# Group statistics of a convolution and state-space kernel: from VectorE's bn_stats to ScalarE's accumulating passes, with the group norms cut into stages

## The chip, the cores and the metric

The kernel runs on one core of a Trainium2 chip. The metric is the device time of one execution in microseconds. The engines are named as the profile names them: PE (TensorE, matmul), PEld (its weight load), DVE (VectorE), ACT (ScalarE), POOL (GpSimd), and SP, whose queue issues most DMAs.

## The reference

Two residual layers work on x of shape (2, 768, 64, 64), in float32:

```python
x = x + _L0_conv_ref(_gn(x), ...)   # layer 0
x = x + _L1_conv_ref(_gn(x), ...)   # layer 1
```

`_gn` is a group norm: each of 32 groups of 24 channels, over all 64 x 64 pixels of an image, has its mean taken away and is divided by sqrt(variance + 1e-5). Layer 0 projects 768 channels to 1536, runs a depthwise 3x3 convolution and SiLU, computes from the result (x_proj) a step size (through softplus) and the vectors B and C of a state-space model with 4 states per channel, scans that model over the 4096 pixels in order, adds D*u, normalizes over channels and projects back to 768. Layer 1 goes through a real 2-D Fourier transform, a two-layer block-diagonal complex MLP with a soft threshold, and the inverse transform.

So statistics per channel are needed three times outside layer 0's first input: of the second image's x (before layer 0 starts on that image), and of layer 0's output of each image (before layer 1).

## The kernel before

**Tiling.** Channels lie on the 128 partitions: 768 are NCT = 6 tiles (`ct`), 1536 are NDT = 12 tiles (`dt`). The 4096 pixels of an image are NCH = 16 chunks of T = 256 (four rows). Layer 0 works through 32 chunks, the 16 of image 0 and then those of image 1.

**Slots.** Layer 0's order is written out by hand (`tc.manual_schedule`). A loop runs over slots t; there are 12 per chunk, 384 in all, and 33 more for the pipeline to drain. In slot t the pieces of a software pipeline are issued for different tiles: `project` (L245, input projection) for tile t, `conv` (L284) and `taps` (L297) for t - 2, `delta` (L341 matmul, L345 Softplus) and `decay` (L352, four exponentials per tile) some 15 behind, `scan` (L369 multiplication, L373 scan), `read` (L382, L383) and `gather` (L388, L390) 17 behind, `output` (L444, output projection) 31 behind, each `ct` in two slots (h = 0 and 1), and `finish` (L455 to L460) in the slot after its second half, so in every odd slot. Every engine takes its instructions strictly in this order.

**Phases.** ScalarE's tables are switched in groups of three slots, phase = t % 3. In phase 2 it runs `root` (L430, L431, once per chunk) and then `silu` (L309) for three tiles; in phase 0 it loads Softplus' table, runs L345 three times, loads the table of Ln and Exp (L551) and starts the exponentials, of which eight fall into phase 1. In the last three slots of a chunk it also normalizes the next chunk's input (L226). `x_proj` (L315) is issued in a phase 2, once per chunk; `x_dbl` (L325) and `spread` (L329, L331) follow in the phase 0 behind it. `moments` (L405) sums for the channel norm in phase 1; `variance` (L420, L422) and `spread_of_tokens` (L427) follow once per chunk.

**Buffers.** PSUM: `pi`, `pc` and `pz` have two banks each, `po` and `mom` one. `pz` serves L341, x_proj, L329, L420 and the group norms in turn. So the third L341 of a phase 0 waits until the first L345 has emptied its bank, and the next `output` waits until L455 has read `po`.

**Statistics.** `prepare` (before the slots) takes bn_stats of image 0's input on DVE (L169). Image 1's input comes in 48 slabs of 128x512: `load_slab` (L147) in slots 40 to 87, `slab_stats` (L150, bn_stats on DVE) one slot later, so in slots 41 to 88. `input_norm(1)` runs whole at the end of slot 91. The output's statistics are a bn_stats (L459) in every `finish`; `aggregate` (L135, six bn_aggr) and the group norm run at the end of slot 223 for image 0 and of slot 415 for image 1.

**The group norm** (L58 to L91) goes back and forth between engines: PE sums the channel means over groups (L64), DVE copies (L77), PE spreads them to the channels (L72), DVE forms the variance parts (L79 to L83), PE sums again (L64), ACT takes Ln and Exp (L87, L88), PE spreads (L72), DVE copies (L90).

**The tail.** From slot 390 on, layer 1's first transform of image 0 (`forward_w`, L616) is issued in pieces between layer 0's last slots: L501 normalizes on ACT, L631 transposes, L639 transforms, and L496/L498 evict on DVE and ACT.

Of the kernel before, what the change touches and what calls it, by code (L numbers as in the profile page):

```python
# [9 lines left out]
F32 = mybir.dt.float32  # L10
AF = mybir.ActivationFunctionType
ALU = mybir.AluOpType
# [3 lines left out]
B, DM, H, W = 2, 768, 64, 64  # L16
L = H * W
DI, NS, R = 1536, 4, 48
G, GC = 32, 24
NCT, NDT = DM // 128, DI // 128  # L20
ROWS = 4
T = ROWS * W
NCH = H // ROWS
# [8 lines left out]
def spectral_kernel(tc, a, out):  # L32
    nc = tc.nc
    x = a["x"]
    xr = x.rearrange("b (ct p) h w -> b p ct (h w)", p=128)
    outr = out.rearrange("b (ct p) h w -> b p ct (h w)", p=128)

    with ExitStack() as top:
        dram = top.enter_context(tc.tile_pool(name="dram", bufs=1, space=DRAM))
        cst = top.enter_context(tc.tile_pool(name="cst", bufs=1))  # L40

        x1_d = [dram.tile([128, NCT, L], F32, name=f"x1_{b}") for b in range(B)]
        y_d = [dram.tile([H, W, DP], F32, name=f"yspec_{b}") for b in range(B)]
        v_d = [dram.tile([H, W, DM], F32, name=f"vspec_{b}") for b in range(B)]

        ident = cst.tile([128, 128], F32, name="ident")
        make_identity(nc, ident)
        sel = cst.tile([128, NCT, G], F32, name="sel")
        nc.sync.dma_start(sel, a["c_sel"])
        selT = cst.tile([G, NCT, 128], F32, name="selT")  # L50
        nc.sync.dma_start(selT, a["c_selT"])
        eps = cst.tile([128, 1], F32, name="eps")
        nc.vector.memset(eps, EPS)

        gm1 = [cst.tile([128, NCT], F32, name=f"gm1_{b}") for b in range(B)]
        gr1 = [cst.tile([128, NCT], F32, name=f"gr1_{b}") for b in range(B)]

        def group_norm(mv, mean, rstd, pool, psum, name):  # L58


            def over_groups(cols, what):
                g = psum.tile([128, 512], F32, tag="pz", name=f"{name}_{what}_g")
                for ct in range(NCT):
                    nc.tensor.matmul(  # L64
                        g[:G, 0:1], sel[:, ct, :], cols(ct), start=(ct == 0), stop=(ct == NCT - 1)
                    )
                return g

            def to_channels(vals, what):
                c = psum.tile([128, 512], F32, tag="pz", name=f"{name}_{what}_c")  # L70
                for ct in range(NCT):
                    nc.tensor.matmul(c[:, ct : ct + 1], selT[:, ct, :], vals, start=True, stop=True)  # L72
                return c

            g = over_groups(lambda ct: mv[:, ct, 0:1], "m")
            gs = pool.tile([G, 1], F32, tag="gn_g", name=f"{name}_gm")
            nc.vector.tensor_copy(gs, g[:G, 0:1])  # L77
            c = to_channels(gs, "m")
            nc.vector.tensor_copy(mean, c[:, :NCT])  # L79
            d = pool.tile([128, NCT], F32, tag="gn_d", name=f"{name}_d")  # L80
            nc.vector.tensor_sub(d, mv[:, :, 0], mean)
            nc.vector.tensor_mul(d, d, d)
            nc.vector.tensor_add(d, d, mv[:, :, 1])  # L83
            g = over_groups(lambda ct: d[:, ct : ct + 1], "v")
            sd = pool.tile([G, 1], F32, tag="gn_g", name=f"{name}_sd")

            nc.scalar.activation(sd, g[:G, 0:1], AF.Ln, bias=eps[:G])  # L87
            root = nc.scalar.activation(sd, sd, AF.Exp, scale=-0.5)  # L88
            c = to_channels(sd, "v")
            nc.vector.tensor_copy(rstd, c[:, :NCT])  # L90
            return root.ins  # L91

        with ExitStack() as ctx:
            layer0(ctx, tc, a, xr, x1_d, y_d, ident, group_norm, gm1, gr1, eps)
        with ExitStack() as ctx:
            layer1(ctx, tc, a, x1_d, y_d, v_d, outr, ident, gm1, gr1)


def layer0(ctx, tc, a, xr, x1_d, y_d, ident, group_norm, gm1, gr1, eps):

    nc = tc.nc
    dram = ctx.enter_context(tc.tile_pool(name="dram0", bufs=1, space=DRAM))
    wp = ctx.enter_context(tc.tile_pool(name="w0", bufs=1))
    st = ctx.enter_context(tc.tile_pool(name="st", bufs=1))
    ps = ctx.enter_context(tc.tile_pool(name="ps0", bufs=2, space=PSUM))
# [19 lines left out]
    gm0 = [st.tile([128, NCT], F32, name=f"gm0_{b}") for b in range(B)]  # L125
    gr0 = [st.tile([128, NCT], F32, name=f"gr0_{b}") for b in range(B)]
    gn0 = [st.tile([128, NCT], F32, name=f"gn0_{b}") for b in range(B)]
    stats1 = st.tile([128, NCT, NCH, 6], F32, name="stats1")
    stats0 = st.tile([128, NCT, 8, 6], F32, name="stats0")
    state = st.tile([128, NDT, NS], F32, name="state")  # L130

    def aggregate(stats, n, mean, rstd, name, pool):
        mv = pool.tile([128, NCT, 2], F32, tag="mv", name=f"mv_{name}", bufs=1)
        for ct in range(NCT):
            nc.vector.bn_aggr(mv[:, ct, :], stats[:, ct, :n, :])  # L135
        group_norm(mv, mean, rstd, pool, ps, name)

    def input_norm(b, pool):
        aggregate(stats0, 8, gm0[b], gr0[b], f"gn0_{b}", pool)
        nc.vector.scalar_tensor_tensor(gn0[b], gm0[b], -1.0, gr0[b], ALU.mult, ALU.mult)  # L140

    slabs = {}

    def load_slab(b, n):
        ct, k = divmod(n, 8)
        slabs[n] = p2.tile([128, 512], F32, tag="xs", name=f"xs_{b}_{n}")
        nc.sync.dma_start(slabs[n], xr[b, :, ct, k * 512 : (k + 1) * 512])  # L147

    def slab_stats(n):
        nc.vector.bn_stats(stats0[:, n // 8, n % 8, :], slabs.pop(n))  # L150

    def prepare():
        with tc.tile_pool(name="xi", bufs=3) as xi, tc.tile_pool(name="wi", bufs=1) as wi:
# [10 lines left out]
            for n in range(2 * NCT):  # L164
                ct, h = divmod(n, 2)
                xs = slabs0[n] if n < 3 else xi.tile([128, 2048], F32, tag="xs", name=f"xs0_{n}")
# [20 lines left out]
            for h in range(2):  # L187
# [5 lines left out]
                    )  # L193
                for dt in range(NDT):
                    nc.vector.tensor_sub(wout[:, dt, half], wout[:, dt, half], wm[:, :384])
            input_norm(0, wi)
            for ct in range(NCT):
                nc.gpsimd.dma_start(
                    wout_d[ct].rearrange("p (dt c) -> p dt c", c=128),
# [2 lines left out]

    p2 = ctx.enter_context(tc.tile_pool(name="p2", bufs=2))
    prepare()
    p1 = ctx.enter_context(tc.tile_pool(name="p1", bufs=1))

    class Chunk:
# [244 lines left out]
        def finish(self, ct):  # L452
            b, i = self.b, self.i
            o = p2.tile([128, T], F32, tag="o", name=f"o_{self.n}_{ct}")
            nc.vector.tensor_mul(o, self.po[ct][:, :T], self.rs)  # L455
            nc.vector.scalar_tensor_tensor(
                o, o, obias[:, ct : ct + 1], self.out[ct][1], ALU.add, ALU.add
            )
            nc.vector.bn_stats(stats1[:, ct, i, :], o)  # L459
            nc.sync.dma_start(x1_d[b][:, ct, i * T : (i + 1) * T], o)  # L460

    chunks = [Chunk(b, i) for b in range(B) for i in range(NCH)]
    N = NDT * len(chunks)

    def at(s):
        return (chunks[s // NDT], s % NDT) if 0 <= s < N else (None, None)

    def both(s, what, *more):
        c, dt = at(s)
        if c is not None:  # L470
            getattr(c, what)(dt, *more)

    S_CONV, S_SCAN, S_OUT = 2, 17, 31
# [4 lines left out]
    for t in range(3):  # L478
        both(t, "load_win")
    both(0, "load_taps")  # L480
    S_TAIL = N + 6

    def tail():
# [41 lines left out]
            evict,  # L525
        )

    with tc.manual_schedule():
        for t in range(N + S_OUT + 2):
            phase, s = t % 3, t - S_SCAN  # L530
            front, fdt = at(t)
            if front is not None and fdt == 0 and t > 0 and t // NDT + 1 < len(chunks):
                chunks[t // NDT + 1].load()
# [27 lines left out]
            o, h = at(t - 1 - S_OUT)  # L561
# [12 lines left out]
            o, h = at(t - S_OUT)  # L574
            if o is not None:
                o.output(h // 2, h % 2)
            o, h = at(t - S_OUT + 3)
# [17 lines left out]
            if front is not None and fdt >= 9 and t // NDT + 1 < len(chunks):  # L595
                for k in range(2):
                    chunks[t // NDT + 1].normalize(2 * (fdt - 9) + k)
            if 40 <= t < 40 + 8 * NCT:
                load_slab(1, t - 40)
            if 41 <= t < 41 + 8 * NCT:  # L600
                slab_stats(t - 41)
            if t == 91:
                input_norm(1, p2)
            if t == S_TAIL:
                spare, given = tail(), 0
            if t >= S_TAIL:
                due = len(spare) * (t + 1 - S_TAIL) // (N + S_OUT + 2 - S_TAIL)
                for do in spare[given:due]:
                    do()
                given = due  # L610
            for b in range(B):
                if t == (b + 1) * NCH * NDT + S_OUT:
                    aggregate(stats1, NCH, gm1[b], gr1[b], f"gn1_{b}", p2)


def forward_w(nc, b, x1, yspec, fw, ident, slab, norm, cols, row, aux, evict):  # L616
# [491 lines left out]
```

## Time and profile before

| | |
|---|---|
| three runs | 4643.34 us median (4640.96 to 4645.46) |
| the profiled execution | 4641.97 us, span 4640.2 us |
| mean granted TensorE clock | 0.978 |
| PE busy | 4388.6 us (95%) |
| DVE busy | 3656.5 us (79%) |
| ACT busy | 2404.2 us (52%) |
| POOL busy | 924.3 us (20%) |
| DMA | 854.38 MB, mean 184 GB/s |
| ACT_TABLE_LOAD | 1.28 us each, 381 of them recorded in the slots |

In the profile's timeline the first scan (L373) starts at 198.4 us and the last at 3338.1; what lies before is `prepare`, what lies behind is the tail and layer 1. Times in the views are microseconds from the span's start. In a group of instructions the numbers behind the bar are busy time and mean nanoseconds of one, and then the engine's idle time before them with what ended it. In a timeline the columns are start, length, engine, line and operation, and in brackets the idle time before and what released it. In a table of stretches each engine has busy microseconds and, in parentheses, instructions, then the granted clock, the DMA share and GB/s.

### The profile page before, as it was taken

To read this page: it belongs to the slowest core of one execution; us is meant where nothing else is said; L and a number is where in the kernel's file an instruction comes from. 1 tells how busy PE (TensorE), PEld (TensorE's weight loads), DVE (VectorE), ACT (ScalarE), POOL (GpSimd) and SP (SyncE) were. 2 spreads that over 40 slices of the span, in tenths; PEclk is the share of its full clock that TensorE was granted. 3 is DMA by queue.
4 is the path that set the end of the run, shared out by engine and by line. 5 is a ranking of instruction groups with operands and counts; after the bars stand their busy time and mean duration, and the time that the engine had idled before them with its cause. 6 is when DMAs were issued, how large, how long until landed. Compare 5 with 4: busy or idle time off the path is not lost.

```text
span 4640.2 us, 78564 instructions
## 1 busy us (share of the span) xinstructions
PE 4388.6 (95%) x28368; PEld 3211.4 (69%) x28368; DVE 3656.5 (79%) x5462; ACT 2404.2 (52%) x4932; POOL 924.3 (20%) x1682
## 2 busy tenths in 40 slices
PE   5999999999999999999999999998779999999997
PEld 4567666777777767777777777775556666777775
DVE  4499999899999999899999999999625555455443
ACT  0365555566556655566665656655634444433331
POOL 1021212122222211122222222222111112212221
PEclk9999999999999999999999999999989999999998
DMA  6566777566666666566666666664574443266646
GB/s 233 181 179 215 220 215 212 175 200 207 200 207 193 195 191 203 174 206 196 196 205 207 204 196 197 200 199 136 191 246 110 120 114 94 60 188 186 169 130 216
DMA packets 521968, 854.38 MB, mean 184 GB/s; under 512 B 61728, under 2 KB 395312, under 8 KB 515056
## 3 DMA queue, kind: packets, MB, share of 16 engines
q1 hardware_dynamic: 518512, 833.73, 59.6%
q0 software_dynamic: 3072, 15.63, 1.0%
q8 instruction: 229, 3.75, 0.3%
q14 instruction: 155, 1.27, 0.1%
HBM read 606.94 MB, written 114.03 MB: 155 GB/s over the span
## 4 chain that ended last, share of the span: by engine, by line
PE 53%; DVE 34%; DMA 5%; ACT 3%; issue 2%; SPq 1%; POOL 1%; DVEq 0%; ACTq 0%; POOLq 0%
DVE hs L373 10%; PE po L444 9%; PE pi L245 9%; PE pc L284 5%; DVE hc L382 5%; DVE hs L369 5%; PE mo L931 4%; PE mo_None L931 4%; DVE pc L297 4%; PE ph L915 3%; PE ph_None L915 3%; DVE u L297 2%; DVE hc L388 2%; PE mz L886 2%; PE mz_None L886 2%
## 5 line engine op out<-in xcount | busy, mean ns | idle before, releaser
L444 PE MATMUL po<-y,wo 128*128 128x256 f32 x4608 | 1079.6, 385 | 60.4 <-DVE o L455 60.4
L245 PE MATMUL pi<-x,wi 128*128 128x256 f32 (+2 forms) x4608 | 1090.2, 386 | 1.1 <-ACT x L226 1.1
L444 PEld LDWEIGHTS po<-y,wo 128*128 128x128 f32 x4608 | 882.1, 192 | 217.7 <-DVE o L455 81.2
L245 PEld LDWEIGHTS pi<-x,wi 128*128 128x128 f32 x4608 | 851.4, 191 | 217.2 <-issue 101.8
L373 DVE TENSOR_TENSOR_SCAN hs<-da,hs 128x1028 f32<-128x1028 f32 x384 | 883.3, 2300 | 46.7 <-DVE hs L369 0.5
L352 ACT ACTIVATE da<-dl,acol 128x256 f32<-128x256 f32 x1536 | 639.6, 497 | 1.8 <-DVE hs L373 0.3
L284 PE MATMUL pc<-pair,wc 128*64 128x256 f32 x4608 | 592.9, 389 | 19.4 <-DMA pair<-win 11.5
L383 POOL TENSOR_TENSOR hc<-hc 128x512 f32<-128x512 f32 x384 | 489.0, 1273 | 613.0 <-DVE hc L382 602.3
L377 POOL COPY state<-hs 128x4 f32<-128x4 f32 x360 | 105.1, 292 | 1984.4 <-DVE hs L373 1984.4
L284 PEld LDWEIGHTS pc<-pair,wc 128*64 128x64 f32 x4608 | 305.2, 136 | 267.5 <-issue 145.8
L260 ACT COPY win<-pi 128x256 f32<-128x256 f32 (+2 forms) x384 | 137.9, 359 | 653.6 <-PE pi L245 622.9
L382 DVE TENSOR_TENSOR hc<-hs,bc 128x1024 f32<-128x1024 f32 x384 | 468.0, 1219 | 0.0
L369 DVE TENSOR_TENSOR hs<-du,bc 128x1024 f32<-128x1024 f32 x384 | 465.7, 1213 | 0.0
L297 DVE SCALAR_TENSOR_TENSOR pc<-win,vec,pc 128x256 f32<-128x256 f32 x768 | 373.8, 487 | 83.1 <-PE pc L284 66.0
L345 ACT ACTIVATE dl<-pz,vec 128x256 f32<-128x256 f32 x384 | 170.4, 473 | 210.3 <-PE pz L341 207.6
L341 PE MATMUL pz<-xd,wdt 128*128 128x256 f32 x768 | 227.7, 405 | 21.9 <-ACT dl L345 20.7
L900 DVE COPY zf_None<-mz_None 32x384 f32<-32x384 f32 (+1 forms) x192 | 100.0, 521 | 184.3 <-ACT zf_None L902 92.7
L900 DVE COPY zf<-mz 32x384 f32<-32x384 f32 (+1 forms) x192 | 100.0, 521 | 175.1 <-ACT zf L902 92.6
L931 PE MATMUL mo_None<-w,hid_None 128*128 128x96 f32 (+1 forms) x1632 | 218.8, 278 | 0.0
L931 PEld LDWEIGHTS mo_None<-w,hid_None 128*128 128x128 f32 (+1 forms) x1632 | 197.2, 188 | 28.0 <-issue 11.4
L924 ACT ACTIVATE hid<-ph,b 128x384 f32<-128x384 f32 (+1 forms) x192 | 106.5, 555 | 211.3 <-PE ph L915 210.0
L931 PE MATMUL mo<-w,hid 128*128 128x96 f32 (+1 forms) x1632 | 214.9, 278 | 0.9 <-DVE v L948 0.9
(147 smaller groups left out, 5540.2 us busy)
## 6 DMA issues: line engine op xcount, KB each, us to landing
wi<-in_win_dram SPq DMA_DIRECT2D x384, 384.0 KB
wo<-wout_d SPq DMA_DIRECT2D x192, 768.0 KB
pair<-win SPq DMA_DIRECT2D x1536, 66.0 KB
wc<-in_wcv_dram SPq DMA_DIRECT2D x384, 192.0 KB
bc<-bc_d SPq DMA_DIRECT2D x32, 1024.0 KB
yspec<-yw SPq DMA_DIRECT2D x64, 512.0 KB
xo<-in_x_dram SPq DMA_DIRECT2D x192, 128.0 KB
x<-o SPq DMA_DIRECT2D x192, 128.0 KB
```

What stands on the lines that cost most here:

```text
L245: nc.tensor.matmul(self.pi[:, : self.tn], self.win[dt][:, ct, :], self.x[:, ct, : self.tn], start=(ct == 0), stop=(ct == NCT - 1),)
L284: nc.tensor.matmul(pc[64 * h : 64 * h + 64, :T], self.wcv[dt][:, h, dx, :], pair[:, h, :, dx : dx + W], start=(dx == 0), stop=(dx == 2),)
L297: nc.vector.scalar_tensor_tensor(acc if dx < 2 else u, wins[dt][:, 2 : 2 + ROWS, dx : dx + W], vec[:, dt, 6 + dx : 7 + dx], acc, ALU.mult, ...
L341: nc.tensor.matmul(pz[:, :T], wdt[:, dt * 128 : (dt + 1) * 128], self.xd, start=True, stop=True)
L352: nc.scalar.activation(das[dt % 4][:, s, 1:], self.dl[dt], AF.Exp, scale=acol[:, dt, s : s + 1])
L369: nc.vector.tensor_mul(hs[:, :, 1:], self.du.unsqueeze(1).to_broadcast([128, NS, T]), self.bc[:, :NS, :])
L373: nc.vector.tensor_tensor_scan(flat, self.da[dt].rearrange("p s t -> p (s t)"), flat, 0.0, ALU.mult, ALU.add)
L382: nc.vector.tensor_mul(hc, hs, self.bc[:, NS:, :])
L383: nc.gpsimd.tensor_add(hc[:, 0:2, :], hc[:, 0:2, :], hc[:, 2:4, :])
L444: nc.tensor.matmul(self.po[ct][:, :T], self.out[ct][0][:, dt, :], self.y[dt], start=(dt == 0), stop=(dt == NDT - 1),)
L915: nc.tensor.matmul(to, w1[rows, self.hp, cols], self.zf[rows, :nt], start=True, stop=True)
L931: nc.tensor.matmul(self.po[:n, j, :], self.hid[:, q, j * 128 : j * 128 + n], w2[:, self.hp, q, :], start=(q == 0), stop=(q == 2),)
```

## The change

bn_stats leaves the slots. In its place ACT makes two passes over a tile: Identity with a bias column (minus a pivot, so that the squares stay small) and Square, each with an accumulator output that gives the sum over the columns. The sums lie per channel, chunk and kind (`sums1` for outputs, `sums0` for image 1's input), and `gather_sums` turns them into mean and variance on DVE with one reduction and four small operations, where six bn_aggr were. The pivot of the outputs is the input's group mean (`pivot1`), that of image 1's input is one pixel of each channel (`pivot0`, a DMA).

`measure` for an output is issued late in the slot of its `finish`. The 48 slabs come one in three slots, from slot 22 to slot 164, instead of one per slot; each one's passes are issued at the end of a phase 2. The group norm becomes a generator, whose pieces are taken one at the end of a phase 1 and one at the start of the phase 2 that follows: image 1's input norm from slot 166 on, image 0's output norm from slot 226 on. The last norm, at slot 415, runs whole as before; so does the one in `prepare`.

```diff
             g = over_groups(lambda ct: mv[:, ct, 0:1], "m")
+            yield
             gs = pool.tile([G, 1], F32, tag="gn_g", name=f"{name}_gm")
             nc.vector.tensor_copy(gs, g[:G, 0:1])
+            yield
             c = to_channels(gs, "m")
+            yield
             nc.vector.tensor_copy(mean, c[:, :NCT])
...
             nc.vector.tensor_add(d, d, mv[:, :, 1])
+            yield
             g = over_groups(lambda ct: d[:, ct : ct + 1], "v")
+            yield
...
-            root = nc.scalar.activation(sd, sd, AF.Exp, scale=-0.5)
+            nc.scalar.activation(sd, sd, AF.Exp, scale=-0.5)
+            yield
             c = to_channels(sd, "v")
+            yield
             nc.vector.tensor_copy(rstd, c[:, :NCT])
...
+    def gather_sums(sums, pivot, mean, rstd, name, pool):
+        mv = pool.tile([128, NCT, 2], F32, tag="mv", name=f"mv_{name}", bufs=1)
+        square = pool.tile([128, NCT], F32, tag="gn_d", name=f"sq_{name}")
+        nc.vector.tensor_reduce(
+            mv, sums.rearrange("p ct n k -> p ct k n"), mybir.AxisListType.X, ALU.add
+        )
+        nc.vector.tensor_scalar_mul(mv, mv, 1.0 / L)
+        nc.vector.tensor_mul(square, mv[:, :, 0], mv[:, :, 0])
+        nc.vector.tensor_sub(mv[:, :, 1], mv[:, :, 1], square)
+        nc.vector.tensor_sub(mv[:, :, 0], mv[:, :, 0], pivot)
+        yield
+        yield
+        yield from group_norm(mv, mean, rstd, pool, ps, name)
+
+    def take_sums(x, sums, pivot, to):
+        nc.scalar.activation(to, x, AF.Identity, bias=pivot, accum_out=sums[:, 0:1])
+        nc.scalar.activation(
+            to, to, AF.Square, accum_out=sums[:, 1:2]
+        )
...
     def slab_stats(n):
-        nc.vector.bn_stats(stats0[:, n // 8, n % 8, :], slabs.pop(n))
+        ct, k = divmod(n, 8)
+        xs = slabs.pop(n)
+        take_sums(xs, sums0[:, ct, k, :], pivot0[:, ct : ct + 1], xs)
...
-            nc.vector.bn_stats(stats1[:, ct, i, :], o)
+            self.o = o
             nc.sync.dma_start(x1_d[b][:, ct, i * T : (i + 1) * T], o)
+
+        def measure(self, ct):
+            sums = sums1[self.b][:, ct, self.i, :]
+            take_sums(self.o, sums, pivot1[self.b][:, ct : ct + 1], junk)
...
+    S_STATS, staged = 22, []
+    S_NORM = S_STATS + 3 * 8 * NCT
+    S_DONE = NCH * NDT + S_OUT + 3
...
+            if t == S_NORM:
+                staged.append(input_norm(1, p2))
+            if t == S_DONE:
+                staged.append(gather_sums(sums1[0], pivot1[0], gm1[0], gr1[0], "gn1_0", p2))
+            if phase == 2:
+                step_of_norm(staged)
...
-            if 40 <= t < 40 + 8 * NCT:
-                load_slab(1, t - 40)
-            if 41 <= t < 41 + 8 * NCT:
-                slab_stats(t - 41)
-            if t == 91:
-                input_norm(1, p2)
+            o, h = at(t - 1 - S_OUT)
+            if o is not None and h % 2 == 1:
+                o.measure(h // 2)
+            n, k = divmod(t - S_STATS, 3)
+            if n == 0 and k == 0:
+                with nc.allow_non_contiguous_dma(reason="one pixel of each channel"):
+                    nc.sync.dma_start(pivot0, xr[1, :, :, 0])
+            if n == 0 and k == 1:
+                nc.vector.tensor_scalar_mul(pivot0, pivot0, -1.0)
+            if 0 <= n < 8 * NCT and k < 2:
+                slab_stats(n) if k else load_slab(1, n)
+            if phase == 1:
+                step_of_norm(staged)
...
-            for b in range(B):
-                if t == (b + 1) * NCH * NDT + S_OUT:
-                    aggregate(stats1, NCH, gm1[b], gr1[b], f"gn1_{b}", p2)
+            if t == N + S_OUT:
+                for _ in gather_sums(sums1[1], pivot1[1], gm1[1], gr1[1], "gn1_1", p2):
+                    pass
```

More of the change, by code (lines that the diff above doesn't have):

```diff
@@ L83, in group_norm @@
             nc.vector.tensor_add(d, d, mv[:, :, 1])
+            yield
             g = over_groups(lambda ct: d[:, ct : ct + 1], "v")
+            yield
             sd = pool.tile([G, 1], F32, tag="gn_g", name=f"{name}_sd")
             nc.scalar.activation(sd, g[:G, 0:1], AF.Ln, bias=eps[:G])
-            root = nc.scalar.activation(sd, sd, AF.Exp, scale=-0.5)
+            nc.scalar.activation(sd, sd, AF.Exp, scale=-0.5)
+            yield
             c = to_channels(sd, "v")
+            yield
             nc.vector.tensor_copy(rstd, c[:, :NCT])
-            return root.ins
         with ExitStack() as ctx:
@@ L127, in layer0 @@
     gn0 = [st.tile([128, NCT], F32, name=f"gn0_{b}") for b in range(B)]
-    stats1 = st.tile([128, NCT, NCH, 6], F32, name="stats1")
+    sums1 = [st.tile([128, NCT, NCH, 2], F32, name=f"sums1_{b}") for b in range(B)]
+    sums0 = st.tile([128, NCT, 8, 2], F32, name="sums0")
+    pivot0 = st.tile([128, NCT], F32, name="pivot0")
+    pivot1 = [st.tile([128, NCT], F32, name=f"pivot1_{b}") for b in range(B)]
+    junk = st.tile([128, T], F32, name="junk")
     stats0 = st.tile([128, NCT, 8, 6], F32, name="stats0")
@@ L135, in aggregate @@
             nc.vector.bn_aggr(mv[:, ct, :], stats[:, ct, :n, :])
-        group_norm(mv, mean, rstd, pool, ps, name)
-    def input_norm(b, pool):
-        aggregate(stats0, 8, gm0[b], gr0[b], f"gn0_{b}", pool)
+        yield
[11 more added lines that the diff above has]
+        nc.vector.tensor_sub(mv[:, :, 0], mv[:, :, 0], pivot)
+        yield
+        yield
+        yield from group_norm(mv, mean, rstd, pool, ps, name)
+    def take_sums(x, sums, pivot, to):
[3 more added lines that the diff above has]
+        )
+    def input_norm(b, pool):
+        if b == 0:
+            yield from aggregate(stats0, 8, gm0[b], gr0[b], f"gn0_{b}", pool)
+        else:
+            yield from gather_sums(sums0, pivot0, gm0[b], gr0[b], f"gn0_{b}", pool)
+        nc.vector.tensor_scalar_mul(pivot1[b], gm0[b], -1.0)
         nc.vector.scalar_tensor_tensor(gn0[b], gm0[b], -1.0, gr0[b], ALU.mult, ALU.mult)
@@ L195, in prepare @@
                     nc.vector.tensor_sub(wout[:, dt, half], wout[:, dt, half], wm[:, :384])
-            input_norm(0, wi)
+            for _ in input_norm(0, wi):
+                pass
             for ct in range(NCT):
@@ L480, in layer0, with step_of_norm @@
     both(0, "load_taps")
+    def step_of_norm(staged):
+        if staged and next(staged[0], staged) is staged:
+            staged.pop(0)
     S_TAIL = N + 6
@@ L610, in layer0 @@
                 given = due
-            for b in range(B):
-                if t == (b + 1) * NCH * NDT + S_OUT:
-                    aggregate(stats1, NCH, gm1[b], gr1[b], f"gn1_{b}", p2)
+            if t == N + S_OUT:
+                for _ in gather_sums(sums1[1], pivot1[1], gm1[1], gr1[1], "gn1_1", p2):
+                    pass
 def forward_w(nc, b, x1, yspec, fw, ident, slab, norm, cols, row, aux, evict):
```

## The prediction

> **What bounds the kernel now.** I read the mean granted clock first (0.978), then the page, the stretches, the groups by shape, the chain, and the timelines of single engines. The page gives PE 95% and DVE 79% busy, but these are means over two layers. The stretches separate them:
>
> ```profile
> 600.00:700.00 100.00, 93.36 (x513) 67.81 (x512) 96.93 (x135) 56.75 (x119) 19.54 (x35) 0.98 0.69 212
> ...
> 1000.00:1100.00 100.00, 99.39 (x563) 73.22 (x562) 96.72 (x135) 58.36 (x120) 21.80 (x38) 1.00 0.66 202
> ...
> 1900.00:2000.00 100.00, 96.97 (x529) 73.74 (x530) 85.17 (x122) 52.00 (x105) 17.31 (x31) 0.92 0.57 173
> ```
>
> The columns are PE, PEld, DVE, ACT, POOL. In layer 0 DVE is at 97% with only its fixed gaps left, PE is close behind, and ACT stands at 55 to 62%. So both DVE and PE have to be counted. DVE's period is read from the chain:
>
> ```profile
> 1005.59 2.30 DVE hs L373
> ...
> 1012.94 2.30 DVE hs L373
> ...
> 1021.58 2.30 DVE hs L373
> ```
>
> There is one scan per slot: 7.35 us without an output to finish, 8.64 with one, 0.35 more in the slot with L427. Twelve slots make 6 x 7.35 + 6 x 8.64 + 0.35 = 96.3 us. The scans twelve apart (1005.6 and 1101.8) say the same, and so does almost every chunk: DVE sets the pace. Now PE, in one slot of phase 0:
>
> ```profile
> 1054.85 1.52 PE L284 MATMUL pc<-pair,wc 128*64 128x256 f32 x12
> 1056.30 1.13 PE L341 MATMUL pz<-xd,wdt 128*128 128x256 f32 x4
> 1057.26 2.75 PE L245 MATMUL pi<-x,wi 128*128 128x256 f32 x12
> 1059.85 0.59 PE L341 MATMUL pz<-xd,wdt 128*128 128x256 f32 x2
> 1060.29 2.75 PE L444 MATMUL po<-y,wo 128*128 128x256 f32 x12
> ...
> 1067.68 2.86 PE L444 MATMUL po<-y,wo 128*128 128x256 f32 x12 [0.40 <-DVE o L455]
> ```
>
> Matmul ends are modelled, so I take start to start: this slot is 8.12 us (the next L284 starts at 1062.97). The other phases, read in the same way where nothing waits: phase 1 with the moments 7.81, phase 2 6.82. Once per chunk come px 2.6, pb 0.6 and pm 0.9. Sum: 4 x (8.12 + 7.81 + 6.82) + 4.1 = **95.1 us of PE per chunk**. The missing 1.2 us are waits like the one shown, for DVE. So PE is only 1.2% behind DVE: whatever DVE loses in a plain chunk, at most 1.2 us of it shows.
>
> **The change, part by part.** The two removed operations:
>
> ```profile
> L459 DVE BATCH_NORM_STATS2 stats<-o 128x6 f32<-128x256 f32 x192 | 82.1, 428 | 6.7
> L150 DVE BATCH_NORM_STATS2 stats<-xs 128x6 f32<-128x512 f32 x48 | 33.0, 688 | 2.6 <-DMA xs<-in_x_dram 2.6
> ```
>
> *L459 leaves DVE.* Six per chunk at 0.43 plus gap: DVE falls from 96.3 to about 93.6, below PE's 95.1. Could DVE's uneven slots still stop PE? The po bank is single, so from one finish to the next DVE may lag some 3.7 us (PE reaches L444 4.1 us into a slot, L455 takes 0.4). Adding pairs of slots (DVE 7.35 + 8.21, PE 14.9 to 17.3) the lag stays below 2 us. I price the chunk at PE's 95.1.
>
> *L150 leaves DVE in slots 41 to 88.* There each slot holds 0.6 us more on DVE, and the scans show 383.6 to 800.0, 416.4 us for four chunks. At PE's pace 4 x 95.1 = 380.4: **-36.0**.
>
> *Plain chunks.* Six from 909.3 to 1486.9 (577.6 to 570.6): **-7.0**. Thirteen from 1989.9 to 3242.0 (1252.1 to 1236.3): **-15.8**. Four around the change of batch, 1486.9 to 1877.7 (390.8): there L245 is 192 or 320 wide, which lets PE run in front and then behind; between 0 and -10.4, I take **-7**.
>
> *The two group norms inside layer 0.* Today each is a chain across engines:
>
> ```profile
> 821.92 1.52 DVE L135 BATCH_NORM_AGGREGATE mv_gn<-stats 128x2 f32<-128x48 f32 x6
> ...
> 829.01 2.71 PE L72 MATMUL gn_v_c<-gn_sd,selT 32*128 32x1 f32 x12 [0.57 <-ACT gn_sd L88]
> ```
>
> The chunks that hold them take 109.3 (800.0 to 909.3) and 112.2 us (1877.7 to 1989.9), against 95.1: **-14.2** and **-17.1**, PE's slower restart included (clock 0.92 in the stretch above). The stages remain as work: PE has L64 twice at 0.8 and L72 twice at 2.7, 7.0 us per norm, and PE is now the bound: **+14.0**. DVE's part (a reduce and a dozen operations at 0.17) fits into its 1.4 us per chunk of room; the copy that opens a slot waits for a stage that closed the slot before, at most some 2.7 us, which the lag above allows.
>
> *What ACT gains.* No accumulating pass is in the trace. Without its sum a pass with a bias column costs like L309, 0.50, and a Square like L397, 0.42. For 512 columns I add 0.23, the difference between L416 (0.59) and L260 (0.36). The sum may cost nothing or one more short instruction, 0.36 at most (the 8x256 copy L331); I take L88's 0.20, since it too is a single column. A pair costs 0.9 to 1.6 us, I take 1.3; a slab 1.4 to 2.1, I take 1.8. That is 6 x 1.3 + 4 x 1.8 = 15 us in a chunk with slabs: ACT goes from about 60 to 76%. Capacity is there; place decides. Phase 2 ends with Silu, then measure and slab, and phase 0 begins with a table load and Softplus, whose buffer PE wants back for the third L341:
>
> ```profile
> 1633.81 1.18 ACT L226 ACTIVATE x<-x,gn,gr 128x320 f32<-128x320 f32 x2
> 1635.01 1.28 ACT L345 ACT_TABLE_LOAD   x1
> 1636.31 0.84 ACT L345 ACTIVATE dl<-pz,vec 128x256 f32<-128x256 f32 x2
> 1639.42 0.47 ACT L345 ACTIVATE dl<-pz,vec 128x256 f32<-128x256 f32 x1 [2.27 <-PE pz L341]
> ```
>
> ACT waits 2.27 us for PE here: that is the cover, with the two L226 already in it. A pair and a slab (3.1) exceed it by 0.9. In the third slot before, without L226, the cover is 3.4 and holds. In the slot with root (L430) PE already waits some 0.4 us for ACT; DVE's L427 will come about 1.4 us earlier, so a slab exceeds it by 0.8. The last, where x_proj follows, has 1.97 us of idle time and hides a slab. So 1.7 us per chunk in the twelve chunks with slabs: **+20** (0 to 50, by the cover and the bounds of the passes). Elsewhere a pair fits: 0.
>
> By the page "ScalarE: Activation LUTs" of the Trainium skill, section "What ACT_TABLE_LOAD costs", an ACTIVATE takes 280 ns with a bias column or 186 ns without, plus 0.833 ns per column; this case agrees for 256 columns (0.50 and 0.42). By it a pair would be 0.9 and a slab 1.3 us, and the +20 would be about +6; what the sum costs is not stated. The same page's "Rules for kernel authors" gives add and multiply to VectorE, not ScalarE, which speaks against this change; here VectorE is at 97% and ScalarE at 58%, and that row outweighs it.
>
> *Small parts.* pivot0 is one DMA of 768 single values, and a DVE multiplication waits for it one slot later with the next scan queued behind it; slots there take 7.4 us, and xs (256 KB) arrives within a slot: 0 to +5, I take +1. Slabs and that DMA go through SP once in three slots instead of every slot, 48 issues of 0.59 us as before, and SP has idle time between slots. Behind slot 390 ACT also normalizes and evicts (19.1 of 20 us busy at 3282 to 3302) and PE waits for it; thirteen pairs cost 0 to 9, less 13 x 0.43 of DVE that is partly on the chain, and the last norm trades L135's 2.8 us for a reduce behind the last pair: I take **+3** (-5 to +9).
>
> Sum: -36.0 - 7.0 - 15.8 - 7 - 14.2 - 17.1 + 14.0 + 20 + 1 + 3 = **-59**. The profiled execution took 4641.97 (span 4640.2 and 1.8 around it), 1.4 below the median of 4643.34; so 4643 - 59, **4584 us**.
>
> **Rivals.** (a) *PE alone, ACT hidden.* The cover is greater than I read, or passes are as short as a plain row: the +20 and the +3 go: 4561. For it: ACT's 40% of idle time. Against: the 2.27 us above. (b) *ACT gives half of it back.* The sums cost 0.36 each and other places in ACT's order reach PE too (L260 behind the eight exponentials of phase 1, then the pair DMA): +50 to +65 instead of +20: 4620. (c) *Slower: the stretch from Silu to Softplus becomes the bound.* Without any cover each added pass between them falls on PE: 48 slabs at 1.8 and some 64 pairs at 1.3, 170 us instead of 20: 4734. It decides from 0.65 us per group of three slots (83 us of gain over 128 groups). A table load for Square behind Silu would do it (1.28 each; the trace shows Square only under the table of Ln and Exp, and L226 after Silu without a load). Against it: in three of the four groups of a chunk the idle time read above (2.27, 3.4, 1.97) is three to five times that. (d) *The norms still stall* because each stage waits in order and PE pays in place: +15 to +20, 4600; within the forecast's upper part. (e) *DVE wasn't the bound*, and only the norms' 17 us go, less the ACT waits: no change, about 4640. Against it: the 96.3 us of scans to 0.1 us in twenty chunks.
>
> **Chances.** Forecast with (d), 4568 to 4605: 0.58. (a): 0.16. (b): 0.12. (e), within 0.2% (9 us, about what a measurement of this kernel can tell from no change): 0.04. (c): 0.10. So faster 0.86, same 0.04, slower 0.10. The range takes in the bounds of the ACT waits and of the tail, reaching into (a) and (b): 4553 to 4622.
>
> **What will show it.** Right: scans 7.3 to 8.2 us apart and twelve of them within 95 to 97 us everywhere, 600 to 700 included; PE without waits for L455; DVE with idle time before L455 or L297, released by PE; no 10 us hole near slots 91 and 223. ACT waits: PE L341 released by ACT L345 in the first fourteen chunks alone. Wrong: more ACT_TABLE_LOAD than the 381 recorded in the slots now; PE waits for ACT in every third slot to the end; accumulating passes over 0.9 us; chunks of 96.3 as before.

## The result, and the profile after

The changed kernel takes **4666.6 us** (median of 6 runs, 4662.6 to 4675.7), the kernel before 4642.5. The ratio is 1.0053, with a 95% interval of 1.004 to 1.0066: slower. The forecast was 4584 (4553 to 4622). The profiled execution has a span of 4661.0 us at a mean granted clock of 0.976.

Lines have moved: L284 is now project's matmul (L245 before), L380 and L384 delta (L341, L345), L412 the scan (L373), L483 and L494 the output matmul and its first reader (L444, L455); L165 and L166 are the two accumulating passes.

Stretches of the changed kernel (PE, PEld, DVE, ACT, POOL, clock, DMA share, GB/s), the first with slabs, the second without:

```profile
600.00:700.00 100.00, 92.80 (x511) 68.11 (x512) 88.09 (x116) 66.09 (x148) 18.92 (x34) 0.98 0.68 196
...
2300.00:2400.00 100.00, 100.00 (x561) 74.75 (x560) 95.47 (x127) 69.09 (x158) 20.91 (x38) 1.00 0.70 206
```

Between 2300 and 2400 all is as forecast: PE is never without work and DVE has room. Between 600 and 700 neither is full: DVE fell from 97 to 88% and PE did not rise. Something else holds both there. The starts of the scans, read from the timelines, give the time by stretch (us):

| slots | before | after | forecast for after |
|---|---|---|---|
| 29 to 172, with slabs | 1198.3 | 1254.5 | 1169 |
| 173 to 232 | 503.0 | 482.1 | 486 |
| 233 to 388 | 1252.1 | 1235.7 | 1236 |
| behind 388 | 1398.2 | 1400.0 | 1401 |

(The forecast's column takes from before's the terms of the prediction that belong to the stretch, each norm's 7.0 in the stretch in which its stages begin.) The first row alone is 85 us above the forecast, a little more than the whole miss; the second is 4 below it. The list of waits (total, times, longest) has a newcomer in these chunks, third below, and with it PE waits four times as long for Softplus as before (21 us then; second line). The first line is DVE waiting for PE:

```profile
DVE o L494 <- PE po L483: 107.1, 40, 5.7
...
PE pz L380 <- ACT dl L384: 87.2, 31, 6.0
...
ACT xs L165 <- DMA xs<-in_x_dram: 75.1, 39, 4.3
```

The chain of waits of the changed kernel from 1125 to 1165 us shows how they hang together:

```profile
1129.96 7.50 DMA xs<-in_x_dram
...
1137.49 0.82 ACT xs L165 x2
...
1138.34 0.72 ACT xs L166 x2
...
1139.08 1.28 ACT L384
1140.38 0.48 ACT dl L384
...
1140.90 0.70 PE pz L380 x2
1141.60 4.28 PE po L483 x12
```

This slab takes 7.5 us from issue to landing. ScalarE reaches its pass over it earlier and stands there, in order; Softplus' table, Softplus and the bank that PE wants back stand behind it. In before, DVE came to the slab 4 to 10 us after its issue (median 7.3), and waited 2.6 us in all, in four places.

### The profile page after: what moved, and what is told of

Read it like the earlier page. It is cut to its first block, busy times and chain, and to the rows that moved or that the text cites. A ratio compares the mean times of both kernels' runs of the same rounds, so it can differ in the third digit from the quotient of the medians.

```text
span 4661.0 us, 79130 instructions
## 1 busy us (share of the span) xinstructions
PE 4390.7 (94%) x28368; PEld 3217.3 (69%) x28368; DVE 3548.6 (76%) x5222; ACT 2664.5 (57%) x5892; POOL 922.4 (20%) x1682
## 4 chain that ended last, share of the span: by engine, by line
PE 73%; DVE 8%; DMA 8%; ACT 6%; SPq 2%; issue 1%; POOL 1%; DVEq 0%; ACTq 0%; POOLq 0%
PE pi L284 16%; PE po L483 16%; PE pc L323 8%; PE mo L995 4%; PE mo_None L995 4%; DMA xs<-in_x_dram 4%; PE pz L380 3%; PE ph L979 3%; PE ph_None L979 3%; DVE hs L412 3%; PE mom L444 2%; PE mz L950 2%; PE mz_None L950 2%; PE px L354 2%; PE py L703 1%
## 5 line engine op out<-in xcount | busy, mean ns | idle before, releaser
L483 PE MATMUL po<-y,wo 128*128 128x256 f32 x4608 | 1084.8, 386 | 19.8 <-DVE o L494 19.8
L284 PE MATMUL pi<-x,wi 128*128 128x256 f32 (+2 forms) x4608 | 1088.2, 386 | 1.1 <-ACT x L265 1.1
L483 PEld LDWEIGHTS po<-y,wo 128*128 128x128 f32 x4608 | 893.3, 194 | 167.5 <-DVE o L494 25.3
L284 PEld LDWEIGHTS pi<-x,wi 128*128 128x128 f32 x4608 | 850.0, 190 | 216.3 <-issue 89.9
L412 DVE TENSOR_TENSOR_SCAN hs<-da,hs 128x1028 f32<-128x1028 f32 x384 | 883.2, 2300 | 46.5 <-DVE hs L408 0.5
L380 PE MATMUL pz<-xd,wdt 128*128 128x256 f32 x768 | 234.8, 415 | 91.3 <-ACT dl L384 87.2
L380 PEld LDWEIGHTS pz<-xd,wdt 128*128 128x128 f32 x768 | 131.7, 193 | 176.2 <-ACT dl L384 109.4
L384 ACT ACTIVATE dl<-pz,vec 128x256 f32<-128x256 f32 x384 | 168.3, 472 | 147.1 <-PE pz L380 145.6
```

What stands on the lines that cost most here:

```text
L284: nc.tensor.matmul(self.pi[:, : self.tn], self.win[dt][:, ct, :], self.x[:, ct, : self.tn], start=(ct == 0), stop=(ct == NCT - 1),)
L380: nc.tensor.matmul(pz[:, :T], wdt[:, dt * 128 : (dt + 1) * 128], self.xd, start=True, stop=True)
L412: nc.vector.tensor_tensor_scan(flat, self.da[dt].rearrange("p s t -> p (s t)"), flat, 0.0, ALU.mult, ALU.add)
L483: nc.tensor.matmul(self.po[ct][:, :T], self.out[ct][0][:, dt, :], self.y[dt], start=(dt == 0), stop=(dt == NDT - 1),)
```

## The experiments

Theory A: the slab's landing, in ScalarE's order, is the loss. Theory B: the passes' own time between Silu and Softplus is. Ten further kernels ran; each ratio is to runs of the kernel before on the same chip, with its 95% interval.

| run | median us | ratio |
|---|---|---|
| the changed kernel | 4666.6 | 1.0053 (1.004 to 1.0066) |
| e1_early_load | 4571.0 | 0.9849 (0.9834 to 0.9864) |
| e2_phase1 | 4553.0 | 0.9807 (0.9792 to 0.9822) |
| e3_wait_alone | 4615.8 | 0.9945 (0.9931 to 0.996) |
| e4_stages_only | 4624.3 | 0.9963 (0.995 to 0.9975) |
| e5_outputs_on_dve | 4590.5 | 0.9883 (0.9868 to 0.9898) |
| e6_slabs_on_dve | 4561.0 | 0.9821 (0.9806 to 0.9835) |
| e7_outputs_alone | 4599.8 | 0.9912 (0.9893 to 0.993) |
| e8_phase1_late | 4597.3 | 0.9901 (0.9885 to 0.9917) |
| e9_ahead_of_wo | 4594.6 | 0.9896 (0.9881 to 0.991) |
| e10_whole_norms | 4571.4 | 0.9846 (0.9829 to 0.9862) |

**e1_early_load**, against the changed kernel:

```diff
-            if 0 <= n < 8 * NCT and k < 2:
-                slab_stats(n) if k else load_slab(1, n)
+            m, j = divmod(t - S_STATS + 3, 3)
+            if 0 <= m < 8 * NCT and j == 0:
+                load_slab(1, m)
+            if 0 <= n < 8 * NCT and k == 1:
+                slab_stats(n)
```

> Only the slab DMAs move: each is issued three slots earlier, the passes stay at the end of phase 2. Theory A (ScalarE stands in order at its first pass over a slab until the slab has landed; 75 us of such waits are in the changed kernel's trace, and they push Softplus and with it PE): the waits go and with them most of the 113 us by which the twelve slab chunks exceed PE's 95.1 us each; 4590 us (4580 to 4605). Theory B (the passes themselves, 1.75 us per slab between Silu and Softplus, are what PE waits for): nothing changes, 4655 to 4670.

It took 4571.0, 96 us less than the changed kernel, and even below A's range. Waits for xs on ACT are gone from the list, and PE's waits for Softplus are down:

```profile
PE pz L380 <- ACT dl L384: 23.4, 18, 4.8
```

A slab chunk now takes 97.0 us (one scan starts at 578.9, the twelfth after it at 675.9, and so, within 0.1 us, for ten chunks in a row). B's share can be no more than 97.0 less 95.1.

**e2_phase1** is e1 with the passes at the end of phase 1, one slot earlier in a group (and so two slots later in time):

```diff
-            if 0 <= n < 8 * NCT and k == 1:
-                slab_stats(n)
+            if 0 < n <= 8 * NCT and k == 0:
+                slab_stats(n - 1)
```

> As e1_early_load, and the passes over the slabs are issued at the end of phase 1, ahead of ScalarE's idle time, not between Silu and Softplus. Theory A: no better than e1_early_load, about 4590. Theory B: the slab chunks fall to PE's 95.1 us each, 4555 to 4570. If both have a part, e1 lies between and this one reaches 4555 to 4570.

4553.0, 2 us below the range given: both have a part, as in the expectation's last case. The slab chunks take 95.1 us, PE's own work, and PE's waits for Softplus shrink to

```profile
PE pz L380 <- ACT dl L384: 8.2, 7, 1.8
```

So the passes between Silu and Softplus cost 18 us (4571.0 to 4553.0), and the wait for the landing 96 on top of them. This is also the fastest version of the study: 1.9% faster than the kernel before, and 2.4% below the changed one's median.

**e3_wait_alone** leaves the wait and takes the passes away, and with them the statistics of image 1's input:

```diff
-        take_sums(xs, sums0[:, ct, k, :], pivot0[:, ct : ct + 1], xs)
+        nc.scalar.activation(
+            sums0[:, ct, k, :], xs[:, 0:2], AF.Identity, bias=pivot0[:, ct : ct + 1]
+        )
```

> The two passes over each slab are replaced by one activation over two columns, at the same place and with the same DMA; the statistics of image 1's input are thereby left out (they come from two pixels of each slab). So the wait for the slab stays and 1.5 us of pass per slab goes. Theory A: most of the loss stays, 4630 to 4650. Theory B: it goes, 4560 to 4580.

4615.8, between the two ranges: neither theory alone. The waits are as long as before the edit, PE's are two thirds:

```profile
PE pz L382 <- ACT dl L386: 59.1, 29, 4.1
...
ACT sums L188 <- DMA xs<-in_x_dram: 80.0, 37, 4.1
```

Taking the passes out of this place gives 51 us where the wait is present and 18 us where it is not (e1 to e2). That is what one cover shared by both would do: the prediction's 2 to 3 us of ScalarE's idle time per group swallow a part of whatever comes first, and more of what comes on top falls on PE. The idle time itself was not varied.

**e4_stages_only** is the kernel before with `group_norm` as the generator of the diff, stepped in the same way; its core:

```diff
             if t == 91:
-                input_norm(1, p2)
+                staged.append(input_norm(1, p2))
+            if t == S_DONE:
+                staged.append(aggregate(stats1, NCH, gm1[0], gr1[0], "gn1_0", p2))
+            if phase == 1:
+                step_of_norm(staged)
```

> The kernel before with one part of the change alone: the two group norms inside layer 0 are taken in stages (from slots 91 and 223 on), all statistics stay bn_stats on DVE. If stages are worth what the prediction says (two chunks of 109.3 and 112.2 us come down to DVE's 96.3 plus the stages' own DVE and PE work, some 2 to 4 us each): 4642 less 20 to 25, 4617 to 4624. Rival: the stages wait in order and stall as before: 4635 to 4642.

4624.3, 17 us below the kernel before on the same chip (4641.5), at the weak end of the range and 0.3 outside. The two chunks that held a norm went from 109.3 and 112.2 to 98.3 and 99.6 us, and the chunk behind each became 0.9 us longer (96.3 to 97.2).

**e10_whole_norms** undoes the stages in e2_phase1, where PE is the bound:

```diff
-            if phase == 1:
-                step_of_norm(staged)
+            if phase == 1 and staged:
+                for _ in staged.pop(0):
+                    pass
...
```

> e2_phase1 with the two group norms inside layer 0 taken whole, at the end of slots 166 and 226. The stages were worth 17 us in the kernel before, where DVE is the bound. If they are worth as much where PE is (a whole norm holds PE for 13.1 and 15.9 us, its own work is 7.0): 4553 + 15 is 4568 (4563 to 4573). If PE pays for the norms in either form: 4550 to 4558.

4571.4, inside the first range, so 18 us lost: the stages are worth about the same with either engine as the bound.

**e5_outputs_on_dve** is e2_phase1 with the outputs' statistics as they were:

```diff
-            self.o = o
+            nc.vector.bn_stats(stats1[:, ct, i, :], o)
...
-            o, h = at(t - 1 - S_OUT)
-            if o is not None and h % 2 == 1:
-                o.measure(h // 2)
...
```

> e2_phase1 with the outputs' statistics put back on DVE (bn_stats in finish, six bn_aggr). Theory: PE's 95.1 us per chunk is the floor of e2_phase1, and DVE's 96.3 becomes the bound again in some 26 chunks: 4553 plus 26 x 1.2 is 4584 (4578 to 4592). Rival: ScalarE's two passes per output cost PE something in the plain chunks too, and without them the loss is smaller: 4555 to 4575.

4590.5, 37 us more than e2_phase1 and as the theory has it; the chunks are at 96.3 us again, slab or not.

**e7_outputs_alone**, the outputs' passes on ScalarE and all else as in the kernel before:

```diff
+            if 40 <= t < 40 + 8 * NCT:
+                load_slab(1, t - 40)
+            if 41 <= t < 41 + 8 * NCT:
+                slab_stats(t - 41)
+            if t == 91:
+                for _ in input_norm(1, p2):
+                    pass
...
```

> One part of the change alone: the outputs' statistics on ScalarE; slabs (one per slot, slots 40 to 88) and whole group norms as in the kernel before. Prediction's terms for that part: plain chunks -7.0 -7 -15.8, DVE-bound slab chunks lose 6 x 0.43 each (103.4 to 100.8), so -10, and the tail +3: 4642 - 37 is 4605 (4598 to 4615). Rival: the passes on the outputs cost as much as they give: 4625 to 4645.

4599.8, 44 us below before and inside the first range: this part of the change is a gain. Plain chunks take 95.1, the slab chunks 101 to 104.

**e6_slabs_on_dve** is e1_early_load with

```diff
-        ct, k = divmod(n, 8)
-        xs = slabs.pop(n)
-        take_sums(xs, sums0[:, ct, k, :], pivot0[:, ct : ct + 1], xs)
+        nc.vector.bn_stats(stats0[:, n // 8, n % 8, :], slabs.pop(n))
...
```

> e1_early_load with the 48 slabs' statistics back on DVE as bn_stats, still one in three slots, the outputs' on ScalarE. DVE then has 93.6 plus 4 x 0.62, so 96.1 us in the twelve slab chunks, and ScalarE nothing between Silu and Softplus: 4553 plus 12 x 1.0 is 4565 (4560 to 4572). Rival: DVE's bn_stats stands in order behind a slab that lands late, as ScalarE did: above 4580.

4561.0, as expected; the slab chunks take 95.9 to 96.3. Once the slabs are spread out and loaded early, it matters little which engine takes their statistics: with DVE the kernel is 10 us faster than with ScalarE behind Silu (e1), and 8 us slower than with ScalarE at its best place (e2).

**e8_phase1_late** is e2_phase1 with late loads:

```diff
-            m, j = divmod(t - S_STATS + 3, 3)
+            m, j = divmod(t - S_STATS - 2, 3)
```

> e2_phase1, but each slab is loaded in the slot before its passes again, as in the changed kernel, so ScalarE waits for it at the end of phase 1, ahead of its idle time of about 5 us. If the wait cost so much only because it stood between Silu and Softplus: 4550 to 4562 although the trace shows waits for xs as long as before. If a wait of ScalarE costs wherever it stands: 4590 to 4620.

4597.3, within the second range: a wait costs there too, but far less of it. The list of waits has

```profile
ACT xs L165 <- DMA xs<-in_x_dram: 208.0, 48, 8.9
```

208 us of waiting for 44 us of time (over e2_phase1), where the changed kernel's 75 us cost 96. The expectation's two cases were too coarse. In two of the four groups of a chunk the waits, of 1 to 4.5 us, vanish in ScalarE's idle time; in one, of about 4 us, PE's L380 behind it waits 0.9 us; and those of 8 us, in the slot before x_proj, outlast the idle time and delay Silu (PE's L354 then waits 1.20 us for L348 at 662.36, and 1.6 on average).

**e9_ahead_of_wo**, the changed kernel with the slab's issue moved within its slot:

```diff
+            m, j = divmod(t - S_STATS, 3)
+            if 0 <= m < 8 * NCT and j == 0:
+                load_slab(1, m)
             o, h = at(t - S_OUT + 3)
             if o is not None and h % 2 == 0:
                 o.load_out(h // 2)
...
```

> The changed kernel with the slab's DMA issued in the same slot, but ahead of load_out (wo, 768 KB) in SP's queue; the passes stay where they are. In the changed kernel's trace ScalarE's turn at a slab came about 7.3 us after the issue where wo had been issued just before, about 4.1 us where it had not. If wo in front of it is what makes a slab land late, the waits of the two slots per chunk that follow a wo fall by some 3 us, and PE's 3.3 and 2.3 us there with them: 4666 less 12 x 4 is 4618 (4605 to 4635). If a slab takes as long wherever it stands in the queue, only the 1.1 us by which it is issued earlier come back: 4640 to 4655.

4594.6, better than either case. In the slots with wo ScalarE now finds its slab landed when it comes, mostly 6.2 us after the issue, where in the changed kernel 7.4 us went by (in 3 of 23 it still waits, 0.7 us at most); what waits are left come from the other slots, where ScalarE comes 0 to 3.6 us after the issue:

```profile
ACT xs L165 <- DMA xs<-in_x_dram: 34.0, 20, 4.0
```

So one line in SP's order, in the same slot, turns the change from 0.5% slower into 1.0% faster.

## Why the prediction was wrong, point by point

- **What bounds the kernel: right.** DVE at 96.3, PE at 95.1 us per chunk. Where nothing of ScalarE interferes, the chunks came down to 95.1 (13 plain ones 1235.7 against the forecast's 1236), and e5 put them back to 96.3.
- **Slabs leave DVE, -36: right as a term.** In e2_phase1 the four chunks from slot 41 take 381.3 us, 35 less than before.
- **The stages of the norms, -31.3 + 14.0 = -17.3: right in direction, and the +14.0 too large.** e4 gives -17 and e10 +18, but e4 has DVE as the bound, where its own expectation asked for 20 to 25, so the agreement with -17.3 is partly luck. The 0.8 and 2.7 us were read in the kernel before while the clock was granted at half:

```profile
820.90:834.40 13.50, 10.21 (x60) 8.30 (x60) 5.79 (x18) 0.45 (x2) 0.26 (x2) 0.50 0.20 56
```

In stages, at full clock, the twelve L72 take 1.43 us start to start and the twelve L64 0.44 (e2_phase1 at 1426.17 and 1399.76). That is 3.7 us per norm instead of 7.0, so the term should have been about +7.5.
- **The passes between Silu and Softplus, +20: right.** 18 us (e1 to e2). The duration too: a pair occupies ScalarE for 1.13 us (forecast 1.3) and a slab for 1.59 (1.8), in the timeline below. In e1, PE's extra waits in slab chunks stand mostly behind the slot with two L265, 1.0 us per chunk, where the prediction put 0.9; behind root 0.1 instead of 0.8. So the total was right, but not for the place with root. (The smaller figure of about +6 beside it comes to about +4 by its own terms: 0.9 and 1.3 fit into 2.27, and the place with root keeps 0.3.)
- **The step that failed** is among the small parts: "xs (256 KB) arrives within a slot", and "slabs and that DMA go through SP once in three slots instead of every slot ... and SP has idle time". It was said of SP's load and of DVE's pivot, and the wait of the first pass over a slab was never priced: the forecast counted ScalarE's time from the end of Silu as if the data were there. "Within a slot" was near enough for DVE, which came to the slab 7.3 us after its issue (median). ScalarE comes to it 2 to 5 us after the issue, and the landing takes 4 us, or 7 where wo was issued just ahead. That term was 0 in the sum and is 96 us. The prediction named what is queued behind a waiting instruction for the pivot ("with the next scan queued behind it") and not for the slabs.
- **Rival (c)** named the place (Silu to Softplus) and the point from which it decides (0.65 us per group), but its causes were a missing cover and a table load. Neither occurred: ACT_TABLE_LOAD stands at 381 in the slots, and the cover was there until the wait took it.
- **The tail, +3: right** (1.8 in the profiled executions).

ScalarE's timeline in the changed kernel, with the lengths of the passes:

```profile
1134.03 0.49 ACT L165 ACTIVATE junk<-o,pivot 128x256 f32<-128x256 f32 x1
1134.43 0.19 ACT L165 ACTIVATION_READ_ACCUMULATOR junk<-o,pivot 128x1 f32 x1
1134.65 0.42 ACT L166 ACTIVATE junk<-junk 128x256 f32<-128x256 f32 x1
1134.97 0.19 ACT L166 ACTIVATION_READ_ACCUMULATOR junk<-junk 128x1 f32 x1
1137.49 0.72 ACT L165 ACTIVATE xs<-xs,pivot 128x512 f32<-128x512 f32 x1 [2.33 <-DMA xs<-in_x_dram]
1138.12 0.18 ACT L165 ACTIVATION_READ_ACCUMULATOR xs<-xs,pivot 128x1 f32 x1
1138.34 0.63 ACT L166 ACTIVATE xs<-xs 128x512 f32<-128x512 f32 x1
1138.88 0.19 ACT L166 ACTIVATION_READ_ACCUMULATOR xs<-xs 128x1 f32 x1
1139.08 1.28 ACT L384 ACT_TABLE_LOAD   x1
```

Why 75 us of waits cost 96 us is read from PE in the twelve chunks with slabs (slots 29 to 172), in the changed kernel and in e1:

```profile
288.70:1543.20 1254.50, 1175.21 (x6392) 868.23 (x6392) 1092.24 (x1461) 839.18 (x1904) 244.17 (x432) 0.98 0.67 195
...
290.80:1453.70 1162.90, 1149.08 (x6387) 850.65 (x6386) 1091.63 (x1460) 834.44 (x1904) 244.99 (x432) 1.00 0.72 210
```

The stretches differ by 92 us. PE is idle 79 us in the first and 14 in the second, 65 more; and for nearly the same count of matmuls it is busy 26 us longer, because after stops the clock is granted at half (below). So about a quarter of the loss is clock. How much of the idle time comes from the cover that passes and waits share is not separated further than by e3.

## What to carry to other kernels

When work that reads a DMA moves to another engine, compare the lead: the time from the DMA's issue to the moment at which the new engine reaches it, against the landing time, behind what else is in the queue. An engine with 40% of idle time is not free at every place; price a wait by what stands behind it in order, and put work that may wait ahead of the engine's own idle time, not between two links of another engine's chain. Issue the load an iteration early: here that alone was worth 96 us. And read the granted clock where a price is taken: work timed just after a stop of PE can be at half clock.

## What the runs showed of the hardware

An accumulator output is an instruction of its own: 0.19 us behind each pass, 0.13 of it visible, as it overlaps the pass's end; 256 and 512 columns take the same.

Where ScalarE waited for it in the changed kernel, a 256 KB load had landed about 4 us after its issue, and 7.4 us (median of 23) when a 768 KB load was issued 1.1 us ahead of it. Issued ahead of the 768 KB load instead (e9), it was there when ScalarE came, mostly after 6.2 us, in 20 of 23 cases, and 6.7 us after the issue at the latest.

A short stop of PE has a price behind it. In the changed kernel's PE timeline:

```profile
1140.90 0.70 PE L380 MATMUL pz<-xd,wdt 128*128 128x256 f32 x2 [2.42 <-ACT dl L384]
1141.44 4.44 PE L483 MATMUL po<-y,wo 128*128 128x256 f32 x12
1145.81 1.52 PE L323 MATMUL pc<-pair,wc 128*64 128x256 f32 x12
1147.25 2.86 PE L284 MATMUL pi<-x,wi 128*128 128x256 f32 x12
```

After 2.42 us of idle time twelve L483 take 4.44 us, not 2.75, and the next groups are at full pace. The stretches of the same moment show the granted clock (the figure before the last two) at half:

```profile
1140.90:1142.20 1.30, 1.30 (x6) 1.17 (x7) 0.33 (x1) 0.86 (x3) 0.00 (x0) 1.00 0.00 0
1142.30:1145.60 3.30, 3.30 (x9) 2.37 (x7) 0.00 (x0) 3.29 (x7) 0.00 (x0) 0.50 0.02 5
1145.70:1152.00 6.30, 6.30 (x35) 4.98 (x35) 5.95 (x7) 3.89 (x11) 0.37 (x2) 1.00 0.64 167
```

In layer 0 of every trace the granted clock is either 1.00 or 0.50, and it stays at 0.50 for 3.41 us or a multiple of that. In the chunks with slabs this adds up to 61.7 us in the changed kernel, 30.7 in e3, 6.8 in e9, 3.4 in e1 and in e2, and none in e8. Dividing each trace from 300 to 1500 us into windows of 3.41 us, in step with these changes of the clock, shows what sets it off: at full clock, each of the 26 windows in which PE was idle for 60% or more (by the profile's busy time) was followed by one at half clock, none of the 4142 with 56% or less was, and between 57 and 59% both occur. So a stop of 2.4 us may cost nothing or 1.7 us of pace, by where it falls (the changed kernel has both: 2.45 us at 929 us without, 2.42 at 1141 with). From 300 to 1500 us the granted clock is 0.97 in the changed kernel and 1.00 in e1 and e2. The Trainium skill's page "TensorE: Matmul & The Clock Gate", Part 1, describes a gate that halves the clock after an idle window of about 3.4 us; the traces agree on the half and on the length, and show that the window need not be idle throughout.
